# Zeros for the scatter target and for a lent region are written during the counting, and the squeeze of the edge list begins at row 14

## The chip, the cores and the metric

The kernel runs on one core of a Trainium2 chip. The metric is device time in microseconds (us) of one execution. Before the change the median of three runs is 3428.38 us (3427.46 to 3428.44).

The engines are named as the profile names them: PE is the matrix engine and PEld its weight loads, DVE the vector engine, ACT the scalar engine, POOL the general engine that issues the indirect gathers, and SP the engine that issues most plain transfers. A letter q behind an engine means its sequencer, for instance a transfer that it issues.

## The reference

A graph layer over 12500 nodes with 256 features and 212500 sorted edges (100000 random ones in both directions, plus one loop for each node), a top-2 mixture of 64 experts, a batch norm and a layer norm:

```python
deg_out = clip(segment_sum(ones, src), 1.0)
deg_in = clip(segment_sum(ones, dst), 1.0)
h = feats * rsqrt(deg_out)[:, None]
m = segment_sum(h[src], dst) * rsqrt(deg_in)[:, None]
x = (m @ W_gc + b_gc) + (feats @ W_res + b_res)
y = x + _moe_ff(x, Wg, bg, w1, b1, w2, b2)      # top 2 of 64 experts, CAP = 1024
y = (y - mean(y, 0)) * rsqrt(var(y, 0) + BN_EPS) * gamma + beta
return _layernorm(feats + y, axis=-1)
```

The edges come sorted by dst, in float32 arithmetic.

## The kernel before

The work goes through five stages.

**Counting (0 to 197 us).** The out-degree of every node is a histogram of src. The edges are taken in 83 groups of 20 columns of 128. For each group DVE builds two one-hot tables (o_hi, o_lo, L202), ACT builds seven more by a sign (s_lo, L410), and PE multiplies them into two accumulators (deg L412, deg_s L414). The buffers of these tables are double. Inside this loop, in program order, small pieces are placed: at group 2 the load of x into the big tile acc (L420), at group 30 columns() (the first 168 columns of edges, loaded into tables, cast by ACT at L278, transposed by PE), at group 40 windows() (the first node of each edge group, from three small loads called begin, L288 to L295, used by DVE at L306), and at group 50 weights() (the weights of the layer, L346 to L357, transposed by PE at L361). In this stage the instruction order on each engine is chosen by a scheduler, not by hand.

**Building h (197 to 245 us).** x is scaled by rsqrt(deg_out) in acc and written to DRAM as h_d (L528). A check of the edge list runs beside it on the tile room. Then acc is set to zero in fourteen pieces (L542, ten on POOL and four on DVE), each after its piece has been written out. All engines read a flag; if edges don't fit the fixed layout, a slow branch (the If at L546) is taken. It is not taken with this input.

**Gather and aggregate (245 to 2320 us).** The edges are laid out as 1584 rows of 128, in 132 groups of 12. For each row, POOL gathers 128 rows of h_d by an indirect transfer into a ring of 6 buffers with 4 rows each (L693), DVE makes a one-hot matrix of the relative target nodes (one_hot, L685, 16 rows ahead, in 5 tiles of 6 rows each), and PE multiplies the two (L707). Finished groups are turned, added into acc, and sent through the dense layer and the routing, with lags counted in rows. From here on PE, DVE, ACT and POOL keep the order of the program (manual_schedule). A heap todo holds steps by the row at which they are due; later(t, f, k) sets a step k lags behind row t (LAG is 11 rows), and at_row(c, f) sets it at row c.

Rows 0 to 167 come straight from the edge list. Rows 168 and on come from a list that is first squeezed: each of 118 partitions takes 1620 edges and leaves out 84 self loops and repeats. The squeeze (compact, compact_by) needs room, and this room is lent by the tail of acc: lent is the last ROOM = 6482 columns, which are written by the aggregation only later. So the zeros in the lent place are first copied to DRAM (lent_d, L590), then lanes.fetch() sets it with three memsets on POOL (L461, L466) and loads src and dst into it (L462, L463); 46 steps on DVE (L474 to L1067) squeeze it; PE transposes the result (lay, L1076), ACT writes it into src_col and rel (laid, L1084, L1087), DVE derives marks; and at last lent_d is read back into the lent place (L1119). In this kernel the 46 steps are spread over rows 0 to 101.

On SP, own(g) loads 128 rows of h_d for each group from the fifteenth on (L735), and best() stores the finished rows of the layer as x2_d (L916).

**Experts (from 2340 us)** gather x2_d by expert and scatter their outputs into z_d. Slots that are never written must be zero, so z_d is filled with zeros by 98 transfers of 256 KB (L615 to L618). These stand in the program behind the If, but depend on nothing, and the scheduler has put them early on SP.

**Finish (to the end):** batch norm, layer norm and output.

Of the kernel before, what the change touches and what calls it, by code (L numbers as in the profile page):

```python
# [8 lines left out]
F32 = mybir.dt.float32  # L9
# [10 lines left out]
P = 128  # L20
N = 12500
D = 256
# [5 lines left out]
NT = (N + P - 1) // P  # L28
NP = NT * P
# [14 lines left out]
GR = 12  # L44
# [5 lines left out]
L = -(-(M - HE) // NL // 2) * 2  # L50
SKIP = L - GR * P
BITS = SKIP.bit_length()
NC = NG * GR
W = P
SL = 64
# [44 lines left out]
def gnn_moe_kernel(  # L100
# [23 lines left out]

    h_d = dram.tile([N, D], F32, name="h_d")
    x2_d = dram.tile([N, D], F32, name="x2_d")
    lent_d = dram.tile([P, 3 * L + 2 * ((L + 2) // 2)], F32, name="lent_d")
    z_d = dram.tile([2 * NP, D], F32, name="z_d")

    def rows(t):  # L130
# [116 lines left out]
    with ExitStack() as stack:  # L247
# [15 lines left out]
        V.memset(bad, 0.0)  # L263
        V.memset(fits[:, 0:1], 1.0)
        V.memset(fits[:, 1:2], 0.0)


        def columns():
# [116 lines left out]
        for c0 in range(0, C0 + 1, CH):  # L385
            n = min(CH, C0 + 1 - c0)
            dig = two.tile([P, CH], I32, name="dig")
            V.tensor_single_scalar(dig[:, :n], src_t[:, c0 : c0 + n], 7, op=ALU.arith_shift_right)
            V.tensor_copy(hi2[:, c0 : c0 + n], dig[:, :n, None].to_broadcast([P, n, 2]))
            dig = two.tile([P, CH], I32, name="dig")  # L390
            V.tensor_single_scalar(dig[:, :n], src_t[:, c0 : c0 + n], 127, op=ALU.bitwise_and)
            k0, k1 = c0 // G, min(c0 + n, C0) // G
            by_g = dig[:, : (k1 - k0) * G].rearrange("p (k g) -> p k g", g=G)
            V.tensor_copy(
                lo2[:, k0:k1],
                by_g[:, :, :GD, None].to_broadcast([P, k1 - k0, GD, 2]),
            )
            V.tensor_scalar(nb[:, k0:k1], by_g[:, :, GD:], -1.0, 0.5, op0=ALU.mult, op1=ALU.add)
            if c0 + n > C0:
                lo_end = sp.tile([P, 1, 2], BF16)  # L400
                V.tensor_copy(lo_end, dig[:, n - 1 : n, None].to_broadcast([P, 1, 2]))  # L401
            for k in range(k0, k1):
                c = k * G
                o_hi = hp.tile([P, G, NT], BF16, name="o_hi")
                hot(o_hi, hi2[:, c : c + G], NT, G)
                o_lo = hp.tile([P, GD, P], BF16, name="o_lo")
                hot(o_lo, lo2[:, k], P, GD)
                s_lo = hp.tile([P, GA, P], BF16, name="s_lo")
                for i in range(GA):
                    S.activation(s_lo[:, i], lane_b, AF.Sign, bias=nb[:, k, i : i + 1])  # L410
                for i in range(GD):
                    T.matmul(deg, o_lo[:, i], o_hi[:, i], start=c + i == 0, stop=False)  # L412
                for i in range(GA):
                    T.matmul(  # L414
                        deg_s, s_lo[:, i], o_hi[:, GD + i],
                        start=c + i == 0, stop=k == whole_groups - 1 and i == GA - 1,
                    )
                if k == 2:
                    for t0, n_t in GROUPS:
                        nc.sync.dma_start(xs[:, t0 : t0 + n_t], whole(x)[:, t0 : t0 + n_t])  # L420
                    nc.sync.dma_start(xs[:RAG, NT - 1], x[(NT - 1) * P :])
                if k == 30:
                    columns()
                if k == 40:
                    windows()
                if k == 50:
                    weights()

        o_hi = hp.tile([P, G, NT], BF16, name="o_hi")
        hot(o_hi[:, :1], hi2[:, C0:], NT, 1)  # L430
# [9 lines left out]

    HALF = (L + 2) // 2
    ROOM = 3 * L + 2 * HALF

    class Lanes:
        def __init__(self, room):
# [64 lines left out]
    with ExitStack() as stack:  # L512
# [33 lines left out]
        with tc.If(unfit > 0):  # L546

            def everywhere(e, n):
                s_c = two.tile([P, 1], I32, name="s_c")
                d_i = two.tile([P, 1], I32, name="d_i")  # L550
                if n < P:
                    V.memset(s_c, 0)
                    V.memset(d_i, NOWHERE)
                for t, v in ((s_c, src), (d_i, dst)):
                    v = v[bass.ds(e, P)] if n == P else v[e : e + n]
                    nc.sync.dma_start(t[:n], v.rearrange("(p c) -> p c", c=1))
                d_c = two.tile([P, 1], F32, name="d_c")
                V.tensor_copy(d_c, d_i)
                r_c = two.tile([P, D], F32, name="r_c")
                GP.indirect_dma_start(  # L560
                    out=r_c,
                    out_offset=None,
                    in_=h_d,
                    in_offset=bass.IndirectOffsetOnAxis(ap=s_c[:, :1], axis=0),
                )
                with tc.For_i(0, NT, 1) as t:
                    o_c = two.tile([P, P], F32, name="o_c")
                    V.tensor_scalar(o_c, lane, d_c, None, op0=ALU.is_equal)
                    V.tensor_scalar_add(d_c, d_c, float(-P))
                    p_c = ps2.tile([P, 4, P], F32, name="p_c")  # L570
                    for h in range(2):
                        T.matmul(
                            p_c[:, h], r_c[:, h * P : (h + 1) * P], o_c, start=True, stop=True
                        )
                    T.matmul(p_c[:, 2, 0:1], o_c, ones_f[:, 0:1], start=True, stop=True)
                    m = acc2[:, :, bass.ds(t * P, P)]
                    V.tensor_add(m, p_c[:, 0:2], m)
                    m = deg_in[:, bass.ds(t, 1)]
                    V.tensor_add(m, p_c[:, 2, 0:1], m)

            with tc.For_i(0, C0 * P, P) as e:
                everywhere(e, P)
            everywhere(C0 * P, RE)
            V.memset(rel[:, :HC], -1.0)
            V.memset(fits[:, 0:1], 0.0)
            V.memset(fits[:, 1:2], -1.0)


    lent = acc[:, 2 * NP - ROOM :]
    nc.sync.dma_start(lent_d, lent)  # L590
    lanes = Lanes(lent)
    lanes.fetch()

# [1 line left out]
    with ExitStack() as stack:  # L595
# [15 lines left out]
            ring.append(r)  # L611

        spare = tables.rearrange("p a b c -> p (a b c)").bitcast(F32)
        zero = spare[:, 3 * D : 5 * D]
        V.memset(zero, 0.0)  # L615
        z_all = z_d.rearrange("(a p r) d -> a p (r d)", p=P, r=2)
        for a in range(NT):
            nc.sync.dma_start(z_all[a], zero)  # L618


        tab = ps1.tile([P, NSLOT], F32, name="tab")
# [10 lines left out]
        def later(t, f, k=1):  # L632
            lag = min(LAG, max(1, (NC - 10 - t) // 12))
            heapq.heappush(todo, (t + k * lag, len(given_at), f))
            given_at.append(t)
# [435 lines left out]
        def lay(j, which, t):  # L1071

            v = (lanes.given[1].bitcast(F32), lanes.buf)[which][:NL]
            q = ps2.tile([P, 4 * P], F32, name="q").rearrange("p (a b) -> p a b", b=P)
            for i in range(4):
                T.transpose(  # L1076
                    q[:, i, :NL], v[:, (j + i) * P : (j + i + 1) * P], ident[:NL, :NL]
                )
            later(t, lambda t: laid(j, which, q, t), 0.5)

        def laid(j, which, q, t):
            to = by_group((src_col, rel)[which])[:, HG:, j : j + 4].rearrange("p g a -> p a g")
            if which == 0:
                S.activation(to, q[:, :, :NL], AF.Copy, scale=fits[:, 0:1])  # L1084
                free_turn(t)
            else:
                S.activation(  # L1087
                    to, q[:, :, :NL], AF.Identity, scale=fits[:, 0:1], bias=fits[:, 1:2]
                )
                free_turn(t)  # L1090
                if j == GR - 4:
                    for i in range(0, NL * GR, 4 * P):
                        later(t + i // P, lambda t, i=i: marks(HC + i))

        def marks(c):
            n = min(4 * P, NC - c)
# [9 lines left out]
        def at_row(c, f):  # L1106
            heapq.heappush(todo, (c, len(given_at), f))
            given_at.append(c)

        def compact_by(c):  # L1110

            steps_of = compact()
            lays = [(j, which) for j in range(0, GR, 4) for which in range(2)]
            c -= 3 * len(lays) + 3 * LAG
            for i, f in enumerate(steps_of):
                at_row(c * i / len(steps_of), lambda t, f=f: f())
            for i, (j, which) in enumerate(lays):
                at_row(c + 3 * i, lambda t, j=j, w=which: hold(t, lambda t: lay(j, w, t)))
            at_row(c + 3 * len(lays) + LAG, lambda t: nc.sync.dma_start(lent, lent_d))  # L1119

        with tc.manual_schedule(engines={
            mybir.EngineType.PE, DVE, mybir.EngineType.Activation, mybir.EngineType.Pool,
        }):
            AHEAD = 16
            fetch(0)
# [400 lines left out]
```

## Time and profile before

| what | value |
|---|---|
| median of three runs | 3428.38 us |
| the profiled execution, its run time | 3428.66 us |
| its span in the profile | 3426.9 us |
| first gather of a row issued | 245.59 us |
| last gather of a row issued | 2284.72 us |
| first gather of the experts issued | 2341.30 us |

The span begins and ends with the profiler's records, and the run time is 1.8 us longer. Lines of groups in the profile read: code line, engine, operation, written tile <- read tiles, count, then busy us and mean ns of one, then the idle time just before them and what ended it. A wait is put down to what released it last. Tables by stage give, for each window, its length, then the busy us and the count in brackets of PE, PEld, DVE, ACT and POOL, then the mean granted clock of PE, the share of the 16 transfer engines, and GB/s.

| stage by the profile, us | PE busy | DVE busy | ACT busy | POOL busy | GB/s |
|---|---|---|---|---|---|
| 20 to 60 | 26.90 | 40.00 | 39.68 | 0.00 | 312 |
| 60 to 100 | 27.90 | 37.73 | 37.51 | 0.00 | 375 |
| 140 to 180 | 31.49 | 40.00 | 37.76 | 0.00 | 1 |
| 220 to 240 | 0.19 | 9.71 | 0.00 | 9.28 | 348 |
| 260 to 280 | 3.73 | 0.00 | 0.38 | 16.18 | 115 |
| 300 to 340 | 19.13 | 39.97 | 0.75 | 35.43 | 49 |
| 500 to 1000 | 395.45 | 240.66 | 45.22 | 379.09 | 126 |

### The profile page before, as it was taken

How to read it: one execution, taken by the hardware profiler on the slowest of the kernel's cores; microseconds unless marked ns; L12 is line 12 of the kernel's file. 1: busy time of each engine (PE TensorE's matmuls, PEld its weight loads, DVE VectorE, ACT ScalarE, POOL GpSimd, SP SyncE). 2: the span in 40 equal slices, each digit the busy share in tenths (PEclk: the TensorE clock that was granted, in tenths of full speed). 3: DMA queues.
4: the chain of work that ended last, by engine and by line, in shares of the span. 5: the costliest groups of instructions: out<-in, count | busy, mean ns of one | idle time of the engine just before them, and what ended most of it. 6: DMA issues, size and time to landing. Idle time of an engine off the chain costs nothing. (4 is left out here: it accounts for less than half of the span.)

```text
span 3426.9 us, 37022 instructions
## 1 busy us (share of the span) xinstructions
PE 2673.9 (78%) x11121; PEld 1782.2 (52%) x11121; DVE 1638.4 (48%) x6013; ACT 707.6 (21%) x1994; POOL 2050.2 (60%) x2092
## 2 busy tenths in 40 slices
PE   6824777887777877887787777876999999999644
PEld 4612344444444544454444444554778766778533
DVE  9976423454445445444454455663222222222498
ACT  8940010000010000000000000111122211222368
POOL 0038877777777777777777777754555555554100
PEclk9756588878898898878888889887999999999865
DMA  9363244444444444444444444433344444556677
GB/s 329 146 222 89 88 152 124 123 124 129 130 126 125 126 127 124 130 129 125 123 129 126 126 126 129 133 95 116 109 132 126 136 151 152 180 179 205 214 223 238
DMA packets 255374, 498.19 MB, mean 145 GB/s; under 512 B 44375, under 2 KB 168789, under 8 KB 246722
## 3 DMA queue, kind: packets, MB, share of 16 engines
q0 software_dynamic: 98800, 264.95, 26.8%
q1 hardware_dynamic: 143072, 218.02, 19.4%
q10 hardware_dynamic: 13298, 12.80, 1.2%
q8 instruction: 91, 1.49, 0.2%
q14 instruction: 113, 0.93, 0.1%
HBM read 402.59 MB, written 96.44 MB: 146 GB/s over the span
## 5 line engine op out<-in xcount | busy, mean ns | idle before, releaser
L693 POOL DMA_INDIRECT ring<-h_d,src_col x1584 | 1552.9, 980 | 495.0 <-issue 424.4
L707 PE MATMUL p<-ring,o 128*128 128x258 f32 x3168 | 1188.8, 488 | 492.0 <-DMA ring<-h_d,src_col 395.0
L707 PEld LDWEIGHTS p<-ring,o 128*128 128x128 f32 x3168 | 622.4, 227 | 973.9 <-DMA ring<-h_d,src_col 633.9
L685 DVE TENSOR_SCALAR o<-lane,rel 128x128 f32<-128x128 f32 x1584 | 376.8, 299 | 602.3 <-PE p L707 602.1
L1222 POOL DMA_INDIRECT xg<-x_d,tables x241 | 233.0, 967 | 336.4 <-PE xtp L1237 219.6
L1266 PE MATMUL yp<-w,h 128*128 128x256 f32 (+3 forms) x1928 | 432.9, 380 | 0.0
L1250 PE MATMUL hp<-xT,w 128*128 128x384 f32 (+11 forms) x1328 | 399.6, 455 | 1.4 <-DVE xT L1241 1.4
L1266 PEld LDWEIGHTS yp<-w,h 128*128 128x128 f32 (+3 forms) x1928 | 341.9, 182 | 64.4 <-issue 7.3
L1254 ACT ACTIVATE h<-hp,w 128x384 f32<-128x384 f32 (+11 forms) x332 | 181.0, 545 | 670.0 <-PE hp L1250 669.3
L742 ACT COPY s<-p 128x258 f32<-128x258 f32 x132 | 49.3, 373 | 1304.4 <-PE p L707 1302.0
L1250 PEld LDWEIGHTS hp<-xT,w 128*128 128x128 f32 x1328 | 248.5, 191 | 131.3 <-issue 56.9
L1272 POOL DMA_INDIRECT z_d<-yo,tables x241 | 238.1, 988 | 121.9 <-DVE yo L1271 65.8
L1241 DVE COPY xT<-xtp 128x768 f32<-128x768 f32 (+2 forms) x83 | 77.4, 932 | 405.2 <-PE xtp L1237 405.2
L1271 DVE TENSOR_TENSOR yo<-yp,bb 128x256 f32<-128x256 f32 (+3 forms) x241 | 102.0, 423 | 276.5 <-PE yp L1266 263.3
L410 ACT ACTIVATE s_lo<-lane_b,nb 128x128 bf16<-128x128 bf16 x581 | 171.0, 389 | 4.4 <-DVE lo_end L401 2.2
L1007 PE MATMUL tab<-at,vals 128*128 128x512 bf16 x392 | 147.1, 468 | 11.1 <-DVE vals L996 11.0
L893 PE MATMUL bank<-wcat,acc 128*128 128x320 f32 x392 | 133.9, 468 | 0.0
L806 DVE TENSOR_TENSOR acc<-q,acc 128x256 f32 x132 | 55.7, 422 | 154.8 <-PE q L783 109.2
L898 PE MATMUL bank<-wcat,xT 128*128 128x320 f32 x392 | 125.9, 445 | 0.0
L461 POOL MEMSET room<- 128x1620 int32 x2 | 2.8, 1446 | 195.4 <-DVE r_out L197 195.4
L702 ACT CAST ring<-mark 128x4 f32<-128x4 bf16 x354 | 57.8, 197 | 260.3 <-issue 260.2
L412 PE MATMUL deg<-o_hi,o_lo 128*128 128x98 bf16 x1079 | 79.7, 235 | 26.8 <-DVE o_lo L202 20.9
(280 smaller groups left out, 2591.1 us busy)
## 6 DMA issues: line engine op xcount, KB each, us to landing
w<-in_wpack SPq DMA_DIRECT2D x64, 1026.0 KB
ring<-h_d,src_col POOLq DMA_INDIRECT x1584
z_d<-tables SPq DMA_DIRECT2D x98, 256.0 KB
zt<-z_d SPq DMA_DIRECT2D x24, 1024.0 KB
tables<-h_d SPq DMA_DIRECT2D x118, 128.0 KB
xt<-in_x ACTq DMA_DIRECT2D x48, 256.0 KB
x_d<-y SPq DMA_DIRECT2D x48, 256.0 KB
z<-in_x SPq DMA_DIRECT2D x12, 1024.0 KB
```

Of the source, the lines that this page charges most:

```text
L410: S.activation(s_lo[:, i], lane_b, AF.Sign, bias=nb[:, k, i : i + 1])
L685: o_last[u] = V.tensor_scalar(o_of[u][:, j], lane, rel[:, c : c + 1], None, op0=ALU.is_equal)
L693: i = GP.indirect_dma_start(out=r[:, k, :D], out_offset=None, in_=h_d, in_offset=bass.IndirectOffsetOnAxis(ap=src_col[:, c : c + 1], axis=0),)
L707: i = T.matmul(p_of[g], o_of[v][:, n], r[:, k], start=j == 0, stop=j == GR - 1)
L893: T.matmul(gps[i][:r], acc2[:, k, a : a + r], wcat[:, k], start=k == 0, stop=False,)
L898: T.matmul(gps[i][:r], v["xT"][:, i, k, :r], wcat[:, 2 + k], start=False, stop=k == 1,)
L1007: T.matmul(tab, vals[:r, m], at[:r], start=t0 + i + k + m == 0, stop=t0 + i == NT - 1 and k + m == 2,)
L1222: GP.indirect_dma_start(out=g, out_offset=None, in_=x2_d, in_offset=bass.IndirectOffsetOnAxis(ap=at[:, 0, k : k + 1], axis=0),)
L1250: T.matmul(hp[:, :m], w1[:, c, j * P : (j + 1) * P], xT[:, c, :m], start=c == 0, stop=c == 1,)
L1254: S.activation(h1[:, j, :m], hp[:, :m], AF.Gelu, bias=w[:, 2 * H + 4 * D + j : 2 * H + 4 * D + j + 1],)
L1266: T.matmul(yp[:r], h1[:, j, k * P : k * P + r], w2[:, j], start=j == 0, stop=j == 3,)
L1272: st = GP.indirect_dma_start(out=z_d, out_offset=bass.IndirectOffsetOnAxis(ap=at[:r, 1, k : k + 1], axis=0), in_=yo[:r], in_offset=None, b ...
```

## The change

The zeros for z_d are issued from inside the counting loop, two transfers for each group from group 4 on, and thirteen more transfers write zeros to lent_d. The copy of the lent place to lent_d stays only in the branch that is not taken. The squeeze begins at row 14 instead of row 0, and its end moves from row 101 to row 109. laid comes 4 rows after lay, and the marks 4 + i rows after that. SP now keeps the order of the program in the gather stage too. The reload of the lent place moves from row 130 to row 138.

```diff
+HALF = (L + 2) // 2
+ROOM = 3 * L + 2 * HALF
...
+        zero = tables.rearrange("p a b c -> p (a b c)").bitcast(F32)[:, 3 * D : 5 * D]
+        V.memset(zero, 0.0)
+        z_all = z_d.rearrange("(a p r) d -> a p (r d)", p=P, r=2)
+        zeros = [(z_all[a], zero) for a in range(NT)]
+        for a in range(0, ROOM, 2 * D):
+            n = min(2 * D, ROOM - a)
+            zeros.append((lent_d[:, a : a + n], zero[:, :n]))
...
+                if 4 <= k:
+                    for o, i in zeros[:2]:
+                        nc.sync.dma_start(o, i)
+                    del zeros[:2]
                 if k == 2:
...
             V.memset(fits[:, 1:2], -1.0)
-    lent = acc[:, 2 * NP - ROOM :]
-    nc.sync.dma_start(lent_d, lent)
+            nc.sync.dma_start(lent_d, lent)
     lanes = Lanes(lent)
     lanes.fetch()
...
-        zero = spare[:, 3 * D : 5 * D]
-        V.memset(zero, 0.0)
-        z_all = z_d.rearrange("(a p r) d -> a p (r d)", p=P, r=2)
-        for a in range(NT):
-            nc.sync.dma_start(z_all[a], zero)
...
-            later(t, lambda t: laid(j, which, q, t), 0.5)
+            at_row(t + 4, lambda t: laid(j, which, q, t))
...
-                        later(t + i // P, lambda t, i=i: marks(HC + i))
+                        at_row(t + 4 + i // P, lambda t, i=i: marks(HC + i))
...
-            c -= 3 * len(lays) + 3 * LAG
+            c -= 3 * len(lays) + 4 + 4 + NL * GR // P + 6
             for i, f in enumerate(steps_of):
-                at_row(c * i / len(steps_of), lambda t, f=f: f())
+                at_row(14 + (c - 14) * i / len(steps_of), lambda t, f=f: f())
...
-            mybir.EngineType.PE, DVE, mybir.EngineType.Activation, mybir.EngineType.Pool,
+            mybir.EngineType.PE, DVE, mybir.EngineType.Activation, mybir.EngineType.Pool, SP,
```

The order of instructions in the two built programs differs as follows. On SP, 54 of the zero transfers now stand ahead of the loads of columns(), 74 ahead of those of windows() and 94 ahead of those of weights(). The users of these loads move too: the cast of columns() stands on ACT behind 39 groups instead of 31, the first use of begin on DVE behind 48 groups instead of 41, and the transposes of weights() on PE behind 54 groups instead of 42. On POOL the three memsets of the lent place stand ahead of the first gather instead of behind the 24th. On SP the loads of the lent place come right behind the If, and the reload of the lent place directly after them.

More of the change, by code (lines that the diff above doesn't have):

```diff
@@ L126, in gnn_moe_kernel @@
     x2_d = dram.tile([N, D], F32, name="x2_d")
-    lent_d = dram.tile([P, 3 * L + 2 * ((L + 2) // 2)], F32, name="lent_d")
+    lent_d = dram.tile([P, ROOM], F32, name="lent_d")
     z_d = dram.tile([2 * NP, D], F32, name="z_d")
@@ L427, in gnn_moe_kernel @@
                     weights()
+        assert not zeros
         o_hi = hp.tile([P, G, NT], BF16, name="o_hi")
@@ L439, in gnn_moe_kernel @@
         rsqrt(sp, r_out, d_out)
-    HALF = (L + 2) // 2
-    ROOM = 3 * L + 2 * HALF
+    lent = acc[:, 2 * NP - ROOM :]
     class Lanes:
```

## The prediction

> **What bounds the kernel now.** The change touches 0 to 470 us, so I ask what paces that stretch and what follows. I began with the waits of POOL, which issues the 1584 gathers (us in total, times, longest):
>
> ```profile
> POOL ring L693 <- issue: 424.4, 1394, 0.3
> ...
> POOL ring L693 <- SPq L727: 12.1, 1, 12.1
> POOL ring L693 <- DMA ring<-h_d,src_col: 4.9, 13, 1.2
> ```
>
> Between gathers stands a fixed 0.30 us and almost nothing else: after the first gather POOL never waits long for anybody. A gather takes 0.945 us undisturbed, so a row costs 1.25 us, and 1584 rows 1980 us of the 2040 us between the first gather (245.59) and the last (2284.72). From 245 to 2286 us POOL is the path. The waits of everybody between 190 and 520 us show what the change aims at:
>
> ```profile
> DVE acc L474 <- DMA acc<-in_dst: 37.2, 1, 37.2
> ...
> PE p L707 <- DVE o L685: 31.1, 3, 24.6
> ```
>
> The first squeeze step blocks DVE for 37.2 us, and PE starves for one-hots behind it. Did POOL notice? Its timeline there (start, length, instruction):
>
> ```profile
> 274.65 0.95 POOL L693 DMA_INDIRECT ring<-h_d,src_col  x1 [0.30 <-issue]
> 275.59 2.85 POOL L461 MEMSET acc<- 128x1620 int32 x2
> 278.37 1.47 POOL L466 MEMSET acc<- 128x1621 bf16 x1
> 280.00 0.95 POOL L693 DMA_INDIRECT ring<-h_d,src_col  x1 [0.16 <-issue]
> ```
>
> No: the 24 slots of the ring took 24 rows while DVE stood, and PE had freed three buffers (rows 0 to 11) before it starved, so POOL could go on to row 35. PE was back at 288.38; POOL at 1.25 us a row would have reached row 36 at about 295. The stall has some 7 us of cover left and costs nothing but the 4.1 us of memsets. What does slow POOL is in the table by stage, restricted to the ring (window, length, busy us and count of PE, PEld, DVE, ACT, POOL, clock, DMA share, GB/s):
>
> ```profile
> 245.00:275.50 30.50, 7.21 (x24) 5.48 (x24) 0.38 (x12) 0.00 (x0) 22.90 (x24) 0.61 0.65 221
> ...
> 287.40:344.00 56.60, 31.56 (x78) 19.07 (x78) 0.00 (x0) 0.00 (x0) 50.02 (x22) 0.65 0.18 51
> 344.00:411.50 67.50, 49.50 (x83) 20.55 (x82) 0.00 (x0) 0.00 (x0) 54.78 (x42) 0.50 0.29 86
> 411.50:470.00 58.50, 35.78 (x82) 15.66 (x82) 0.00 (x0) 0.00 (x0) 43.57 (x47) 0.76 0.49 160
> ```
>
> The fifth pair is POOL. While DVE squeezes, a gather takes 50.02/22 = 2.27 and then 54.78/42 = 1.30 us instead of 0.945: an excess of 29.2 and 15.1 us, 44.3 us on the path. Two timelines, POOL first, show how:
>
> ```profile
> 360.48 2.42 POOL L693 DMA_INDIRECT ring<-h_d,src_col  x1 [0.30 <-issue]
> ```
>
> ```profile
> 360.24 1.84 DVE L1051 TENSOR_TENSOR acc<-acc 118x1620 int32<-118x1620 int32 x1
> ```
>
> The gather that begins inside a squeeze step ends 0.82 us after it. Here rule and row part. The Trainium skill (SBUF — State Buffer, section Who interferes with whom) infers that tensor_tensor takes only the shared read interface, while descriptor generation needs the write interface, so that only copies, casts and tensor_scalars of a 2-port mode hold up a gather. Of the 46 steps those are 14 of about 1.0 us; they cannot make 44 us. By the rule the placing of the tensor_tensors would be worth nothing; I follow the row, by which every step counts.
>
> **Part 1, zeros during the counting.** The pace is a group of 2.025 us on DVE (o_hi every 2.02 to 2.03 us), with ACT as full; the transfers are beside it. SP before:
>
> ```profile
> 37.74 0.36 SPq L275 DMA_DIRECT2D tables<-in_src  x1
> ...
> 48.13 68.63 SPq L618 DMA_DIRECT2D z_d<-tables  x98
> ```
>
> A zero transfer costs 68.63/98 = 0.70 us at full bandwidth. The 98 for z_d are not moved onto the path: they ran from 48 us already. The 13 new ones are 3.24 MB, 8.8 us at 370 GB/s, into a time (120 to 197 us) where the table shows 0 to 2 GB/s: no cost. The memset of zero already stood early on DVE.
>
> The danger is the order on SP. x has moved by about 43 us (DMA share 0.70 in 40 to 44). 54 zeros more bring the loads of columns() to 43 + 54 x 0.70 = 81 us. Their cast ran at 73.57 behind 31 groups; behind 39 it is due at 73.57 + 8 x 2.025 = 89.8: 8 us of cover. 20 more zeros: the loads of windows() at about 97 and, as they took 4.6 us before, there by 102; first use was 97.6, seven groups later is 111.8: 10 us of cover. 20 more: weights() at about 116, 4 us of issuing, there by 122; PE's transposes at 100.0 move 12 groups, to about 124 or a little more: 2 to 5 us of cover, the thinnest. A rule speaks against this change: by the skill (DMA: Bandwidth & Descriptors, Queues, rings and completion order) descriptors of one ring are taken in order, so a small load issued behind bulk waits for it. The row of before puts no bulk but x ahead of them. By the rule alone, with the users where they were, columns() would be late by 81 - 73.6 = 7 us and weights() by 22; with the users' new places the sum is the covers above, so I take no stall.
>
> Moving these blocks also changes where PE falls behind: groups 33 to 44 took 34.1 us (o_hi from 75.16 to 109.29), 9.8 more than 12 x 2.025, of which about 2 are digits that DVE makes anyway. In the new order PE interleaves the two accumulators for 3 groups after columns() instead of 10 (about 0.4 us each, a gain of 3), but weights() no longer lies inside the stall of windows() (a loss of 3 to 4). I take +0.5, between -4 and +4.
>
> **Part 2, the lent place.** The copy out (SP, 0.35 us to issue, 3.24 MB) leaves the path of nobody: POOL never waited for a transfer more than 1.2 us. The memsets cost 4.1 us between two gathers now; they'll cost 4.3 ahead of the first gather, but can begin at the If's end (DVE leaves it at 244.6) instead of after SP's read at 245.59. Sum -0.5, between -1 and +1. The loads behind them land 8 to 10 us later (issue at 277.08 to use at 286.22 now), so at about 257.
>
> **Part 3, squeeze from row 14.** DVE has 30 one-hots (5 tiles of 6) before it needs PE to finish row 5. Gathers begin at 249, row 5 is issued by 256.5 and multiplied some 4 us later (the last gather ends at 2285.67, its matmul begins at 2289.20): the squeeze begins at about 261, its data are there, the stall is gone. Late next is again the gather: DVE needs about 2.0 us for a step and its two one-hots (1.6 + 0.4), and steps come every 95/46 = 2.07 rows or 2.6 us at the least. So DVE is never behind, and all 46 steps run in the loose way of 344 to 411 us. There 18 steps (27.2 us) cost 15.1 us: 0.84 a step, 0.56 per us. Before, 27 steps (44.2 us) ran packed, at 29.2: 1.08 and 0.66. New excess 46 x 0.84 = 39 by count, or 73.3 x 0.56 = 41 by time; I take 41, since the early steps are the longer ones (the scan takes 3.52): -3.5. If steps meet gathers as often as when packed, 73.3 x 0.66 = 48: +4. If they fall oftener into the 0.30 us gaps, say 0.45 per us: -11.
>
> **Part 4, the end of the squeeze.** The last lay is now due at row 124 and laid at 128; POOL can be at row 168 only when PE has done 144: 16 rows, 20 us or more. The reload at row 138 has until the aggregation reaches the tail of acc, beyond row 700. SP by hand keeps the same order of L735 and L916 in the steady part. Cost 0, within 1 us.
>
> **Sum.** 0.5 - 0.5 - 3.5 = -3.5 on the profiled 3428.66 us (1.8 above its span; its median is 3428.38): 3425 us.
>
> **Rivals.**
> 1. The stall was on the path and the squeeze comes 25 us earlier (286 to 261): 3403 us. For it: 37 us is the longest wait of DVE. Against: POOL's timeline has no gap. 6%.
> 2. Same mechanism, larger: 0.45 per us (-11) and a counting shorter by 2: 3415 us. For it: a quarter of each row is a gap in which a step blocks nobody. Against: the rate of 344 to 411 us was measured with just such gaps. 19%.
> 3. Slower: the small loads come late in the counting, at the cast on ACT, the first use of begin and PE's transposes, and hold all three engines one for one. It decides where a zero takes more than about 0.75 us for weights(), 0.85 for columns(). At 0.87: 94 x 0.17 = 16 late, minus 5 of cover, minus the 3.5: 3436 us. The new loads beside x, which runs at 349 GB/s rather than 370, speak for it; 22%.
> 4. The change doesn't do what it says: the data of the squeeze come later than row 14. Up to 25 us of delay would again be hidden by the ring; this lies inside my forecast.
>
> **Numbers.** Forecast 53%. 0.2% is 6.9 us, about what can be told from no change here; faster 0.06 + 0.19 = 0.25, same 0.53, slower 0.22. The forecast's own bounds, -11 and +8, and the middle of rivals 2 and 3 give 3414 to 3437.
>
> **What will show it.** First gather near 249; DVE without the wait of 37 us, first squeeze step near 261; the excess of gathers between there and the last step near 41 us; the counting's end (first use of r_out, 197.27) within 4 us; no wait on tables, begin or wcat. I am wrong if the gather's first row moves by more than 5 us, or the excess leaves 33 to 48 us.

## The result and the profile after

After takes 3422.89 us (median of 20 runs, 3420.68 to 3425.31), before 3428.41 (20 runs beside them): a ratio of 0.9984, interval 0.9977 to 0.9991, so 5.5 us less. That is clear of the noise, and inside the 6.9 us that the prediction calls no change. The profiled execution has a span of 3421.9 us against 3426.9. All stage times below are read from such traces: the start of a named instruction in one execution against that in another.

| milestone, us | before | after | change of the stretch that ends here |
| --- | --- | --- | --- |
| scaling of x begins (first use of r_out) | 197.27 | 194.54 | -2.73 |
| first gather | 245.59 | 246.66 | +3.80 |
| gather of row 167 | 504.53 | 499.69 | -5.91 |
| last gather (row 1583) | 2284.72 | 2282.63 | +2.75 |
| first expert gather (xg) | 2341.30 | 2336.12 | -3.09 |
| end of the span | 3426.9 | 3421.9 | +0.2 |

The changed kernel's lines lie 9 to 16 lower in the code: the gather of L693 is L702, its matmul L707 is L716, the one-hot L685 is L694, the first squeeze step L474 is L490, the memsets L461 and L466 are L477 and L482. The waits of POOL (us in total, times, longest):

```profile
POOL ring L702 <- issue: 424.6, 1394, 0.3
...
POOL acc L477 <- DVEq L562: 11.2, 1, 11.2
```

POOL is the path between 246 and 2284 us as before, with the same fixed gap of 0.30 us. Its one long wait is at the end of the If (before 12.1 us, put down to SP's read at L727; now 11.2 us, put down to DVE's read of the flag at L562). It now stands ahead of the memsets, and so the timeline of POOL shows them ahead of the first gather (start, length, instruction):

```profile
241.97 2.98 POOL L477 MEMSET acc<- 128x1620 int32 x2 [11.24 <-DVEq L562]
244.89 1.59 POOL L482 MEMSET acc<- 128x1621 bf16 x1
246.66 1.16 POOL L702 DMA_INDIRECT ring<-h_d,src_col  x1 [0.17 <-POOL acc L482]
```

The memsets cost 4.6 us here and no longer 4.1 us between gathers 24 and 25. In the waits of all engines between 190 and 520 us the 37.2 us of DVE for in_dst are gone; what DVE waits for now is PE, in short pieces:

```profile
DVE o L694 <- PE p L716: 114.4, 27, 6.7
```

The squeeze's first step on DVE's timeline:

```profile
258.36 0.29 DVE L694 TENSOR_SCALAR o<-lane,rel 128x128 f32<-128x128 f32 x1 [6.71 <-PE p L716]
258.64 1.85 DVE L490 TENSOR_TENSOR acc<-acc 118x1620 bf16<-118x1620 int32 x1
```

DVE comes to it 27.6 us earlier than before (286.22), and POOL gains almost none of that. The table by stage, restricted to the ring:

```profile
245.00:275.50 30.50, 14.83 (x36) 8.35 (x36) 0.00 (x0) 0.00 (x0) 22.75 (x21) 0.67 0.44 129
275.50:344.00 68.50, 45.88 (x80) 19.27 (x80) 0.00 (x0) 0.00 (x0) 56.92 (x39) 0.56 0.26 75
344.00:411.50 67.50, 46.60 (x79) 19.34 (x80) 0.00 (x0) 0.00 (x0) 55.32 (x41) 0.52 0.28 81
```

The fifth pair is POOL: 22.75/21 = 1.08, 1.46 and 1.35 us a gather. Before, the first stage had 24 gathers at 0.95 and the next two (from 287.4 us on) 2.27 and 1.30. The slowing has moved and spread. Its sum, the time of the first 168 gathers beyond 0.945 us each, is called the excess from here on: 43.5 us after and 45.5 before.

### The profile page after: what moved, and what is told of

Same layout as the page of the kernel before. It is cut to its first block, busy times and chain, and to the rows that moved or that the text cites. A ratio compares the mean times of both kernels' runs of the same rounds, so it can differ in the third digit from the quotient of the medians.

```text
span 3421.9 us, 36966 instructions
## 1 busy us (share of the span) xinstructions
PE 2685.0 (78%) x11059; PEld 1778.3 (52%) x11121; DVE 1641.3 (48%) x6013; ACT 707.9 (21%) x1994; POOL 2051.2 (60%) x2092
## 3 DMA queue, kind: packets, MB, share of 16 engines
q1 hardware_dynamic: 144800, 218.02, 19.5%
## 5 line engine op out<-in xcount | busy, mean ns | idle before, releaser
L702 POOL DMA_INDIRECT ring<-h_d,src_col x1584 | 1553.8, 981 | 483.3 <-issue 424.6
L716 PE MATMUL p<-ring,o 128*128 128x258 f32 x3168 | 1207.3, 492 | 473.2 <-DMA ring<-h_d,src_col 436.8
L716 PEld LDWEIGHTS p<-ring,o 128*128 128x128 f32 x3168 | 619.0, 227 | 976.8 <-DMA ring<-h_d,src_col 666.0
L694 DVE TENSOR_SCALAR o<-lane,rel 128x128 f32<-128x128 f32 x1584 | 380.8, 303 | 617.4 <-PE p L716 617.3
L1016 PE MATMUL tab<-at,vals 128*128 128x512 bf16 x330 | 130.2, 471 | 18.2 <-DVE vals L1009 7.7
L477 POOL MEMSET room<- 128x1620 int32 x2 | 2.8, 1447 | 192.7 <-DVE r_out L199 192.7
```

The lines of the kernel that those rows point to most:

```text
L694: o_last[u] = V.tensor_scalar(o_of[u][:, j], lane, rel[:, c : c + 1], None, op0=ALU.is_equal)
L702: i = GP.indirect_dma_start(out=r[:, k, :D], out_offset=None, in_=h_d, in_offset=bass.IndirectOffsetOnAxis(ap=src_col[:, c : c + 1], axis=0),)
L716: i = T.matmul(p_of[g], o_of[v][:, n], r[:, k], start=j == 0, stop=j == GR - 1)
L1016: T.matmul(tab, vals[:r, m], at[:r], start=t0 + i + k + m == 0, stop=t0 + i == NT - 1 and k + m == 2,)
```

## The experiments

The twelve runs went to three chips. On the last one before takes 3428 us as above. On the two others it takes 3716, and this has to be known to read their totals: there PE is granted a lower clock in the gather, and PE, not POOL, paces rows 168 to 1583. Their first 410 us are like those of the other chips and are compared by stage.

### Before and after once more: how far a stage repeats

Nothing is edited.

> The kernel before once more, nothing changed: how far do the stages of one execution repeat? Theory A (the change acts in three places only: counting, lent place, squeeze; the 2.75 us that rows 168 to 1583 took longer and the 3.1 us that the tail from the last gather to the first expert gather took less belong to the execution, not to the change): scaling of x begins at 197.3 +- 0.3, first gather at 245.6 +- 0.3, row 167 issued at 504.5 +- 1, but rows 168 to 1583 (1780.19) and the tail (56.58) differ from the first profile by 1 us or more. Rival (both are made by SP's order written out by hand): these two repeat within 0.5 us as well.

This is the kernel before, on a chip where it takes 3716 us. The stages did not repeat as expected: scaling began at 194.37, not 197.3, the first gather at 243.15, row 167 at 512.20; the excess is 46.0. The tail (last gather to first expert gather) took 60.8 us; rows 168 to 1583 are paced by PE there and say nothing on the question. Why the total is higher is seen in POOL's waits between 600 and 2286 us of this run (remote: a release to which the profile gives no instruction)

```profile
POOL ring L693 <- remote: 115.9, 45, 4.0
POOL ring L693 <- PE p L707: 85.4, 48, 4.4
```

and in its window of that stage (clock third from the end):

```profile
600.00:2200.00 1600.00, 1053.73 (x3725) 727.05 (x3726) 677.78 (x3329) 130.93 (x545) 1064.22 (x1113) 0.75 0.38 111
```

POOL issues 1113 gathers there, and waits up to 4.4 us at a time; the same window of the changed kernel on the last chip has a clock of 0.87 and 1273 gathers:

```profile
600.00:2200.00 1600.00, 1237.95 (x4271) 744.02 (x4270) 789.41 (x3822) 148.76 (x623) 1212.56 (x1273) 0.87 0.43 127
```

> The changed kernel once more, beside the others of this call. Theory A: scaling of x begins at 192.4 to 194.5 (six runs with zeros in the counting lay there; three without lay at 194.4 to 197.3), first gather near 246, squeeze's first step near 258, excess of the first 168 gathers 41 to 46 us. The change's worth: about 5 us where the gathers are the bound; where PE's granted clock in the gather is near 0.74 and PE is the bound (before takes 3716 there) the counting's part and the earlier rows are kept, so 2 to 6 us as well. Rival (the 5.5 us were the clock of one chip): within 1 us of before.

The changed kernel took 3422.99 us beside 3428.07 before (ratio 0.9986, interval 0.9977 to 0.9995): the 5 us repeat. Scaling at 193.40, first gather at 245.72, excess 43.5 again, rows 168 to 1583 in 1781.85, tail 53.84.

### Part 1: zeros during the counting, and the three blocks alone

```diff
-        for a in range(NT):
-            nc.sync.dma_start(z_all[a], zero)
...
+                if 4 <= k:
+                    for o, i in zeros[:2]:
+                        nc.sync.dma_start(o, i)
+                    del zeros[:2]
```

> The kernel before with part 1 alone: zeros for z and lent_d issued two a group during the counting, their old loop gone; copy out, memsets between gathers 24 and 25, and squeeze from row 0 stay. Theory A (counting gains by where the scheduler now puts the three blocks): scaling begins near 194.5 (-2.7), the first gather near 242.9, the 37 us wait of the first squeeze step stays and costs nothing, excess of gathers 44 us; in all -2.7, about 3425.7. Rival (the counting's 2.7 us is chance): 197.3, 3428.4. Rival (SP freed of 98 zeros lets the squeeze's data land earlier): the copy out and its loads no longer share the DMA engines, the wait is shorter than 37 us by 5 to 10, still no time from it.

Scaling at 193.32, the 37.2 us wait still there, excess 46.6; the time 0.9999 (0.999 to 1.0007). So no gain of the whole can be told, where 2.7 us were expected, though scaling begins 1.05 us earlier than in before on that chip. The rival's shorter wait for the data did not come.

```diff
-                if k == 30:
+                if k == 38:
...
-                if k == 40:
+                if k == 46:
...
-                if k == 50:
+                if k == 54:
```

> The kernel before with columns(), windows() and weights() issued at groups 38, 46 and 54 in place of 30, 40 and 50, so that their uses stand where the zeros push them (cast at group 39, transposes of weights at 54 to 56), zeros where they were. Theory A (the counting gains because weights() no longer shares PE with windows() and the two accumulators alternate for 3 groups, not 10): scaling of x begins at 192.4 to 194.5. Rival (the gain is from SP or the DMA, or is chance): it begins at 195 to 197.3.

Scaling at 194.47, at the late edge of the first expectation; the time 0.9992 (0.9983 to 1.0001), again no gain that can be told. Over all traces the start of scaling was 192.4 to 194.5 in ten executions with zeros in the counting, mean 193.4; 197.27, 197.15 and 194.37 in three with the old counting. What goes with this is in the windows of the counting, of before

```profile
80.00:110.00 30.00, 24.35 (x231) 20.15 (x231) 27.35 (x52) 24.46 (x84) 0.00 (x0) 0.59 1.00 376
```

of the run with four copies below, whose counting is the old one too (scaling at 197.15),

```profile
80.00:110.00 30.00, 24.57 (x234) 19.84 (x234) 27.63 (x53) 24.89 (x86) 0.00 (x0) 0.62 1.00 374
```

and of before once more (194.37):

```profile
80.00:110.00 30.00, 25.62 (x254) 19.06 (x252) 29.06 (x55) 26.34 (x92) 0.00 (x0) 0.77 0.99 377
```

At a clock of 0.59 in the stretch of the three blocks DVE's o_hi waits 2.6 us for PE in the whole counting (1.8 for deg_s, 0.8 for deg); at 0.77 it waits 0.7. After waits for none, after once more 0.4. So some 2 us of the 2.73 are PE waits that the changed kernel does not have, and that before does not have in every execution. Seven of the ten executions with zeros show the same 0.77 in this window, and scaling begins there at 192.4 to 193.9, 193.3 in the mean. At that clock, then, the new places are worth about 1 us, by one trace of the old counting against seven of the new. The rest goes with the lower clock, and why it was lower in two of three old countings stays open. The clock of this window is not all either: after has 0.89 in it and, at 194.54, the latest start of the ten.

### Part 2: the lent place ahead of the gather

```diff
-    nc.sync.dma_start(lent_d, lent)
...
+            nc.sync.dma_start(lent_d, lent)
```

The added line stands in the If, and the zeros are moved as in part 1.

> Parts 1 and 2: as the run before, and the lent place is not copied out but in the If, its memsets and loads come ahead of the first gather; squeeze from row 0, lay and marks as before. Theory A (the ring hides a stall of DVE, so its length is worth nothing): the wait of the first squeeze step falls from 37 to some 8 us, first gather near 246.6, no 4.1 us of memsets between gathers, packed squeeze from about 258, excess of gathers 42 to 46 us, in all -3, about 3425.4. Rival 1 (the stall is on the path): the 29 us that the wait loses come off the time, about 3398.

```profile
250.54 1.85 DVE L489 TENSOR_TENSOR acc<-acc 118x1620 bf16<-118x1620 int32 x1 [2.30 <-DMA acc<-in_dst]
```

DVE's wait for data falls from 37.2 to 2.3 us, more than expected: the first step begins 7.6 us after the first of its loads was issued (242.90). Rival 1 falls: the time is 0.9990 (0.9982 to 0.9999), 3.2 us less and not 29. First gather at 246.12, excess 43.3.

### The stall lengthened

```diff
-    nc.sync.dma_start(lent_d, lent)
+    for _ in range(4):
+        nc.sync.dma_start(lent_d, lent)
```

> The kernel before, with the copy of the lent place out to DRAM issued four times in place of once: 9.7 MB more ahead of the squeeze's data, some 27 us at 360 GB/s. Theory A (the ring of 24 slots, and three buffers that PE frees, cover a stall of DVE of about 37 + 7 us): the wait of the first squeeze step grows to 60 to 66 us, the gathers stand still for 17 to 22 us near row 36, and the time grows by about 20 us. Rival 1 (the stall is on the path whatever its length): gathers stand still in before too and here longer by the whole 27 us. Rival (a stall is hidden at any length): no gap between gathers over 5 us, no time.

The three further copies cost 5.6 to 5.9 us each, not the 9 expected: DVE's wait grew by 16.9 us against before once more and 17.6 against before, to

```profile
DVE acc L474 <- DMA acc<-in_dst: 54.8, 1, 54.8
```

and POOL's timeline at last shows it:

```profile
294.10 2.85 POOL L461 MEMSET acc<- 128x1620 int32 x2
296.87 1.47 POOL L466 MEMSET acc<- 128x1621 bf16 x1
309.80 3.37 POOL L694 DMA_INDIRECT ring<-h_d,src_col  x1 [11.46 <-PE p L708]
```

The memsets here stand behind the gather of row 35. The gather that waits 11.46 us is that of row 36, the row that the prediction named. Some 17.2 us more of stall and 11.5 of wait leave some 6 us that the ring still covered. The time grew by 12.4 us (1.0032, 1.002 to 1.0044). So the stall of before was hidden, with about 6 us to spare.

### Part 3: the squeeze from row 0

```diff
-                at_row(14 + (c - 14) * i / len(steps_of), lambda t, f=f: f())
+                at_row(c * i / len(steps_of), lambda t, f=f: f())
```

> The changed kernel with the squeeze from row 0 in place of row 14, all else as changed. Theory A (DVE's stall is hidden by the ring; row 14 only avoids it): DVE reaches the first step near 250 and waits some 7 us for its data; no gap between gathers over 2 us before row 100; steps 110/46 = 2.4 rows apart; excess 41 to 46, row 167 and the time within 2 us of the changed kernel's. Rival (row 14 is what brought the squeeze's 2 us): row 167 comes 2 us or more later than in the changed kernel, excess 45 to 48.

Here my theory fell. The data come almost in time (a wait of 2.87 us), no gap opens, and yet the excess is 46.6 and row 167 comes 4.4 us after that of the changed kernel once more (0.8 us of it before the first gather). The time is 3425.99 us (3424.10 to 3429.25) against 3422.99 (3419.84 to 3426.32) on the same chip. DVE's timeline shows where the slowing begins:

```profile
253.89 1.84 DVE L491 TENSOR_TENSOR acc<-acc 118x1619 bf16<-118x1619 int32 x1
255.65 0.48 DVE L694 TENSOR_SCALAR o<-lane,rel 128x128 f32<-128x128 f32 x2
256.04 1.00 DVE L492 TENSOR_TENSOR acc<-acc 118x1619 bf16<-118x1619 bf16 x1
256.95 0.67 DVE L694 TENSOR_SCALAR o<-lane,rel 128x128 f32<-128x128 f32 x3
257.54 1.84 DVE L493 SCALAR_TENSOR_TENSOR acc<-acc 118x1619 bf16<-118x1619 bf16 x1
```

For its first rows DVE has one-hot tiles to spare, so nothing holds it back, and steps due at rows 0 to 14 run without a pause: rows 0 to 19 have 12.6 us of excess against 3.9. From row 14 on DVE is tied to PE and so to POOL's pace. So the start at row 14 brings about 3 us in this pair, and not by a stall that it avoids.

The packed beginning alone does not explain them. The run with parts 1 and 2 above also starts at row 0 and packed, with 13.2 us of excess in rows 0 to 19, and ends with 43.3, as low as the changed kernel. It ran on another chip and ends its squeeze at row 101. The edit here moves the start and with it the distance of the 46 steps, 110/46 = 2.4 rows in place of 95/46 = 2.1. Which of these costs the 3 us stays open.

### What a step costs: more of them, and fewer

```diff
                     lambda: V.tensor_tensor(b, w, m, op=ALU.bitwise_and),
+                    lambda: V.tensor_tensor(b, w, m, op=ALU.bitwise_and),
+                    lambda: V.tensor_tensor(b, w, m, op=ALU.bitwise_and),
```

> The changed kernel with the AND of each of the seven rounds of shifts made three times (b = w AND m, the same values again): 14 more tensor_tensors of 1.84 us on int32, 60 steps in the same rows. Theory A (every step beside the gathers costs 0.59 us per us, or 0.95 us by count): 14 x 1.84 x 0.59 = 15 or 14 x 0.95 = 13 more of excess: 57 to 59 in place of 43.5, and so much more time where the gathers are the bound. Rival (the skill's inference, tensor_tensor takes only the shared read interface and does not hold up descriptor generation): excess stays at 43 to 45.

Excess 53.1 against the 43.5 that the changed kernel had on the last chip, the last step begins at 422.3 in place of 412.9 us: 9.6 us for 14 tensor_tensors, 0.69 each, 0.37 per us of DVE. That is less than the 13 to 15 us expected, but far from the 0 to 1.5 us that the rival by the skill's inference gives. The whole stood at 1.0004 of before (0.9995 to 1.0014).

The other way round, 14 of the 46 steps are made on room, before the gather, while DVE waits for h_d's stores; only the finished words go out and back into the lent place, so POOL's memsets there and the second load of edges go too:

```diff
-            out_steps = lanes.leave_out(n_left) + [
...
+        for f in words(lanes):
+            f()
+        nc.sync.dma_start(word_d, lanes.given[0][:NL])
...
-    lanes.fetch()
+    nc.sync.dma_start(lanes.given[0][:NL], word_d)
```

> The changed kernel, but the first 14 of the 46 squeeze steps (23.7 us of DVE) are taken out of the gather: the 5 that fitting makes anyway are not made twice, the other 9 are made on the room tile behind fitting, where DVE waits for h_d's stores from 224 to 242 us; only the words (0.76 MB) go out to DRAM and back into the lent place, so POOL's three memsets ahead of the first gather and both loads of edges go; POOL makes all memsets of acc. Theory A (every squeeze step beside the gathers costs 43.5/73.3 = 0.59 us per us): 23.7 x 0.59 = -14 in the gather, first gather 4 us earlier (near 242.3): -18 in all, about 3405. Rival (the skill's inference: only [...]casts and tensor_scalars of a 2-port mode hold up descriptor generation; tensor_tensor does not): of the 14 only four such (4.5 us) go, the gather's excess falls by 4 to 5 us, in all -8, about 3415. Rival (DVE becomes the bound ahead of the If, or the ring waits for the store of the words out of the place it takes over): first gather at 246 to 249, in all -10 to -14.

Excess 33.0, so 10.5 us less, where the rival by the skill's inference had 4 to 5. But the last rival holds too, and more than it said: the first gather came only at 259.50, since the ring's first memset waited for the store:

```profile
DVE ring L658 <- DMA word_d<-room: 16.9, 1, 16.9
```

The time is 3711.01 us, 0.9985 of before (0.9978 to 0.9991). The window of that store, 118 rows of 6480 bytes:

```profile
242.00:258.00 16.00, 0.00 (x0) 0.00 (x0) 0.00 (x0) 0.00 (x0) 0.00 (x0) 0.50 0.13 49
```

With all 128 rows, and the pool of the small tiles reserved ahead of the ring's:

```diff
-        nc.sync.dma_start(word_d, lanes.given[0][:NL])
+        nc.sync.dma_start(word_d, lanes.given[0])
...
+        two = inner.enter_context(tc.tile_pool(name="s_two", bufs=2))
         one = inner.enter_context(tc.tile_pool(name="s_one", bufs=1))
```

> The run with the words made ahead of the gather had the first gather held to 259.5 us by the store of the words: 118 rows went out at 45 to 54 GB/s (DMA share 0.13), and the ring lies where the room was. Here the words go out and back with all 128 rows, and the pool of the small tiles is reserved first, so that the ring lies clear of them. Theory A (each squeeze step beside the gathers costs about 0.95 us of POOL): first gather near 242.5, excess of the first 168 gathers about 32 (43.5 - 14 x 0.83 as that run showed it), row 167 issued near 242.5 + 168 x 1.245 + 32 = 484 where the gathers are the bound; against before some -20 in all, about 3408 where before takes 3428. Rival (the store is slow for another reason than its 118 rows): DMA share stays near 0.13 for 15 us, the squeeze's first step comes near 280 again. Rival (PE is the bound of the gather, as on the chip where before took 3716): row 167 comes early, but the last gather is within 5 us of before's, and the whole gains 5 us or less.

```profile
240.00:244.00 4.00, 0.00 (x0) 0.00 (x0) 1.07 (x6) 0.00 (x0) 0.00 (x0) 0.50 0.54 214
```

The share of the transfer engines is 0.54 and the store is over in 4 us. Two things were edited here; but in the last run below the pools have their old order, and the store of 128 rows is fast as well (0.85 and 344 GB/s from 238 to 240 us). First gather at 245.05 and not 242.5, since the ring's first memset still waited 2.9 us for the store; excess 30.7, so 12.8 us for 14 steps of 23.7 us. The time is 0.9951 (0.9938 to 0.9965), 18 us, on a chip where PE paces the gather: the rival that expected 5 us or less there was wrong. Row 167 came 19.5 us earlier than in before once more, and the last gather 23.5: PE begins its long stretch earlier and ends it earlier.

Four more steps moved, with ACT scaling ten groups of x:

```diff
-            if i % 3 == 1:
+            if i % 3 < 2:
...
-        ]
+        ] + shifts(w, m, b, range(1))
```

> As the run before, and the first of the seven rounds of shifts (4 steps, 6.5 us) is made ahead of the gather as well, in the 8.9 us of DVE that come free because ACT scales ten of the fifteen groups of x instead of five. Theory A: 4 steps less beside the gathers, 3.5 us less than the run before, first gather at the same time within 1 us (DVE done with the words near 240, ACT with scaling near 222). Rival (ACT's scaling holds up the stores of h_d): first gather 3 to 8 us later, the gain is gone.

First gather at 243.60, excess 27.4, the time 0.9939 (0.9926 to 0.9953), 23 us less.

Last, the same 18 steps with the words in the tables, which nobody uses between the counting and row 24, and with the pools in their old order:

```diff
+        word = tables.rearrange("p a b c -> p (a b c)").bitcast(F32)[:, :L]
+        lanes = Lanes(one.tile([P, ROOM], F32, name="room"), word)
```

> As the run with 18 steps made ahead of the gather, but the words lie in the tables, which are free between the counting and row 24, so that the tiles of the gather, the ring among them, do not wait until the words are stored (there DVE waited for that store until 242.2 and the first gather began at 243.6). Theory A: the first gather begins when POOL leaves the If, 240.5 to 241.5, 2 to 3 us earlier, and the whole is so much faster: 24 to 27 us less than before. Rival (something else holds the first gather, as the clearing of the accumulator's last part): 243 or later, no gain over the 23 us of that run.

```profile
242.05 1.18 POOL L758 DMA_INDIRECT ring<-h_d,src_col  x1 [4.01 <-DVE o L750]
243.53 0.96 POOL L758 DMA_INDIRECT ring<-h_d,src_col  x1 [0.30 <-issue]
```

3403.30 us (median of 5) against 3428.07, 0.9930 (0.9916 to 0.9943): 25 us less than before and 20 less than the changed kernel, the fastest of all. First gather at 242.05, 1 us later than expected (it waits for DVE's first one-hots), excess 27.5.

## Why the prediction was right, point by point

**Time.** 3425 was forecast, 3422.9 measured: less than the 6.9 us taken as no change, in the direction of the sum. In part that is luck: the counting came 3.2 us better than its term, with the wrong sign forecast, and the squeeze about 1.6 us worse, and the two errors partly cancel.

**What bounds the kernel** held: POOL from the first gather on. "The stall costs nothing" held: e3 (parts 1 and 2) takes 35 us from it and gains 3; e7 (four copies) lengthens it and pays from row 36 on. "Some 7 us of cover" measured about 6. Rival 1 is refuted by both.

**Part 1**, +0.5 forecast, -2.73 in the pair of traces: inside the bounds of -4 to +4, but the value taken was wrong. The step that failed is the balance of a gain of 3 from less alternating on PE against a loss of 3 to 4 because weights() no longer lies inside the stall of windows(). The waits of o_hi for PE, 2.6 us, are gone; the loss didn't appear: DVE's one wait for PE around weights(), bias for wl_p, is 1.1 us against 0.9 before. The term also scatters by some 3 us with the clock in the counting (194.37 and 197.27 for the same kernel). No wait on tables, begin or wcat appeared, as said, and rival 3 found nothing to begin on. SP's timeline after shows the small loads behind the bulk:

```profile
36.62 39.43 SPq L431 DMA_DIRECT2D z_d<-tables  x54
76.09 0.46 SPq L286 DMA_DIRECT2D tables<-in_src  x1
```

A zero took 39.43/54 = 0.73 us to issue. The loads of columns(), windows() and weights() were issued at 76.1, 91.5 and 107.1 us, 5 to 9 us earlier than the sums had them, and used at 89.6, 109.6 and 126.7: there was more cover than forecast.

**Part 2**, -0.5 forecast. The first gather is 52.12 us behind the scaling in place of 48.32, +3.80; with the 4.1 us that left the gather, -0.3. Right. Of the loads I said that they land 8 to 10 us behind the memsets, at about 257. The 8 us were right (7.6 in e3 and 8.2 in e10, the squeeze from row 0, from the first issue to the first step), but the loads were issued near 243, before the memsets had ended, and in e3 the data were there at 250.54: a slip without a price.

**Part 3**, -3.5 forecast, -1.8 (row 167 less the memsets) to -2.0 (excess) measured. The mechanism was right, steps that slow the gathers beside them, and the first step came at 258.64 (261 said). The size: 41 us of excess forecast, 43.5 measured twice; for before, 44.3 was read from two windows, and all 168 gathers have 45.5. The mis-sized term is the rate per step, 0.84 or 0.56 per us, taken from the window of 344 to 411 us. Over all 46 steps it was 43.5/46 = 0.95 and 43.5/73.3 = 0.59. Where the gain lies was not foreseen either: e10 puts 3 us on the start at row 14 with no stall to avoid, and the cause of that is open, as said there.

**The rule.** Against an inference of the Trainium skill (SBUF — State Buffer, Who interferes with whom) I followed the row, that tensor_tensor holds up a gather too; e8 (the AND three times) bears this out with 9.6 us for 14 of them. The same section also says that an instruction with two inputs in SBUF contends with a GpSimd instruction that reads SBUF; whether that is what a gather meets, no run here shows.

**Part 4**, nothing forecast. The tail's -3.09 and the +2.75 of rows 168 to 1583 look like the work of SP's order and are not shown to be. The same gather code as before, SP not by hand, took 1782.43 us for those rows and 54.65 for the tail in e11 (blocks later), beside 1780.19 and 56.58 in before; after took 1782.94 and 53.49, after once more 1781.85 and 53.84. So the +2.75 came without that order too. Within a tail the clock falls differently on the same instructions, PE's timeline before

```profile
2296.22 2.34 PE L893 MATMUL bank<-wcat,acc 128*128 128x320 f32 x4
2298.36 2.34 PE L898 MATMUL bank<-wcat,xT 128*128 128x320 f32 x4
```

and after:

```profile
2293.27 2.18 PE L902 MATMUL bank<-wcat,acc 128*128 128x320 f32 x4
2295.29 1.24 PE L907 MATMUL bank<-wcat,xT 128*128 128x320 f32 x4
```

Up to 2 us of the tail's difference are therefore open between the clock and SP's order; no run undid that order alone.

## What to carry to other kernels

Before removing a long wait, ask what the engine that sets the pace was doing meanwhile: 37 us of DVE's wait were worth about 3 at most, and 20 us came from 18 steps taken out of the paced stage into an idle stretch of the same engine ahead of it (16 of them from the gathers' excess). Work that is merely hidden beside a paced engine is not free if it slows each of its instructions; what helps is to do less of it there, more than to spread it. And take a stage's scatter from a second trace of the same kernel before giving a few us in it a cause.

## What the runs showed of the hardware that was not expected

- The same kernel took 3428 us on some chips and 3716 on others, with clocks of 0.87 and 0.75 for PE in the gather, and with another engine as the bound; the excess of the gathers beside the squeeze was nearly the same on both (old gather code: 45.5 and 45.4 against 46.0 and 46.6 us).
- A store of 118 rows of 6480 bytes ran at 49 GB/s with 0.13 of the transfer engines' time; with 128 rows it took 4 us at 214 GB/s (0.54).
- DVE's tensor_tensors on int32 slowed the issue of indirect gathers: 14 added ones cost 9.6 us; 18 removed steps of all kinds gave back 16 (43.5 to 27.5).
